# A two-layer graph-attention kernel on one core: the order of work on each engine is read from a sorted table of places instead of from a planner that uses such a table as priorities

## The chip, the cores and the metric

One core of one Trainium2 chip runs the program. The metric is the time of one execution in microseconds (us), on the device. The engines of a core work side by side, each through its own list of instructions in order: TensorE (PE, with PEld for its weight loads), VectorE (DVE), ScalarE (ACT), GpSimd (POOL) and SyncE (SP). SP and POOL here do little but issue transfers (DMA).

## The reference

The input `x` holds 32 graphs of 512 nodes with 512 features, and `adj` their 512 x 512 adjacency. Two attention layers follow each other, all in float32:

```python
def gat_layer(x, mask, W, a_src, a_dst, bias, concat):
    xl = (x @ W).reshape(B, N, H, F)
    asrc = jnp.einsum('bnhf,hf->bnh', xl, a_src)
    adst = jnp.einsum('bnhf,hf->bnh', xl, a_dst)
    e = jax.nn.leaky_relu(asrc[:, :, None, :] + adst[:, None, :, :], 0.2)
    e = jnp.where(mask[..., None], e, -1e9)
    attn = jax.nn.softmax(e, axis=1)
    out = jnp.einsum('bsdh,bshf->bdhf', attn, xl)
    out = out.reshape(B, N, H * F) if concat else out.mean(axis=2)
    return out + bias

h = jnp.maximum(_layernorm(x, axis=-1), 0.0)
mask = (adj > 0) | jnp.eye(N, dtype=bool)[None]
h = jax.nn.elu(gat_layer(h, mask, W1, att_src1, att_dst1, b1, concat=True))    # 4 heads of 256
return x + gat_layer(h, mask, W2, att_src2, att_dst2, b2, concat=False)        # 1 head of 512
```

## The kernel before

The kernel works on one graph after the other and overlaps them: while one graph goes through its second layer, the next goes through the first and the one after that is loaded and normalised. A loop over the graphs (`for i in range(B - 1)`, L1611) records jobs for such a **turn**; 28 of the turns consist of the same 470 jobs each. What stands before them is the start, what stands behind is the end. Nothing is issued while jobs are recorded: `Program.add` only notes for each job its engine, a cost in us and the earlier jobs it depends on, which it derives from the buffers read and written. At the end `Program.emit` issues them in the sequence that `Program.order` returns, and that sequence sets each engine's list.

Most of the matrix products are cut into two by two blocks and done with seven products instead of eight; one of the seven products of the first projection is cut once more. That is why there are many sums and differences on VectorE (`hs`, `hs4`, `t`, `hx`, `wx`, and others in place), and why results pass between PSUM banks by ScalarE copies (`mm<-mm`).

The names that the steps use:

- `mm`: the eight PSUM banks. `ht`: the normalised graph, transposed; `w1_sb`, `w2_sb`: the weights. `xl`, `xl2`: the projected features of layer one and two.
- `as`: the source scores of all nodes on every partition. VectorE transposes them out of `z` (`as<-z`), SP writes them to DRAM (`das<-as`) and reads them back on all partitions (`as<-das`). ScalarE then makes the scores `l<-as,z`, VectorE masks them (`l<-l,mt`) and ScalarE takes their exponentials with sums (`l<-l,low`).
- `rr`: what normalises them goes the same way (`drr<-rr`, `rr<-drr`). VectorE makes `p<-rr,z` from it, GpSimd adds the mask from DRAM by a transfer that accumulates (`p<-dm`), and ScalarE takes `p<-p,z`, the attention weights that TensorE reads.
- `h`: the output of layer one. ScalarE copies it out of a bank with the bias (`h<-mm,b_sb`), VectorE adds the other bank, `xr<-h` and `h<-xr,h` make the ELU.
- `x`: four tiles of the next graph, with `stats<-x` on VectorE; they also serve as scratch for three of the sums of layer two. `t`: four scratch tiles, the residual input and the output of layer two.

The list of an engine is fixed when the program is built. `Program.order` before the change plays the jobs through: it holds each engine's free time, the two transfer queues with their speeds, alone and side by side (`KIND`, `MASK`), the delays between engines (`PAIRS`, `CROSS`, `SAME`), and whenever an engine is free in this play it takes, of the jobs that are ready by then, the one with the smallest rank. The ranks are the numbers of `PLACES` in hundredths of a us, one for each of 2374 jobs: those of the start, of one turn and of the end. A job of turn i has the rank of its place plus i times TensorE's work of a turn. `LATE`, extra lateness of single transfers, is an empty table.

Of the kernel before, what the change touches and what calls it, by code (L numbers as in the profile page):

```python
# [44 lines left out]
class Banks(Slots):  # L45
# [17 lines left out]
PLACES = (  # L63
# [153 lines left out]
)  # L217
LATE = {
   
}  # L220


class Program:
# [7 lines left out]
    CROSS, SAME = 0.15, 0.07  # L231
# [43 lines left out]
    def kind(self, j):  # L275

        if self.jobs[j][0] == "POOL":
            return self.MASK
# [1431 lines left out]
```

## Time and profile before

| | |
|---|---|
| Time, median of 3 runs | 2771.11 us (2768.26 to 2773.03) |
| Profiled execution, its own time | 2769.33 us |
| Its span, first to last instruction | 2767.6 us |
| Instructions | 42320 |
| Transfers | 502.14 MB, 181 GB/s over the span |
| Granted TensorE clock | 0.999 of full |

The span runs from the first to the last instruction, and the execution's own time is 1.7 us longer. Of TensorE's matmuls a weight load (PEld) and a matmul (PE) stand in the profile each; a product in float32 is two of them. Their ends are modelled and overlap the next one's start, so the busy share of PE is nearly 1 also where short pauses are hidden; how far apart the starts are, and how many stand in a stretch, tells more.

The page's largest groups are matmuls, with a mean of 367 to 388 ns each; VectorE's and ScalarE's operations on 128x512 take 681 to 742 and 716 to 721 ns. The chain that ended last is TensorE's for 13% of the span and does not reach back to the start, so I read waits and single places rather than the chain.

### The profile page before, as it was taken

The numbers are of one execution on the slowest core, as the hardware profiler recorded it, in microseconds if no ns is written. First come the engines' busy times: TensorE is split into PE (matmuls) and PEld (weight loads), VectorE is DVE, ScalarE is ACT, GpSimd is POOL, SyncE is SP. The second block draws the span as 40 slices with busy tenths as digits, with TensorE's granted clock in tenths as the row PEclk, the third lists the DMA queues.
The fourth block names the chain that finished last, engine by engine and source line by source line (L and its number), as shares of the span: only waits on it lengthen the run. The fifth ranks groups of instructions, "written<-read, shape, count | busy, mean of one in ns | idle before, by whom it ended". The sixth has DMA issues, their size and how long they took to land. (4 is left out here: it accounts for less than half of the span.)

```text
span 2767.6 us, 42320 instructions
## 1 busy us (share of the span) xinstructions
PE 2742.4 (99%) x12924; PEld 2371.8 (86%) x12924; DVE 2558.2 (92%) x6732; ACT 2229.1 (81%) x4907; POOL 313.1 (11%) x356
## 2 busy tenths in 40 slices
PE   7999999999999999999999999999999999999999
PEld 6788888888888888888888888888888888888887
DVE  8999999999999999999999999999999999999996
ACT  5978888778887788877888877888778788788883
POOL 0110111101111111111011111111111111101110
PEclk9999999999999999999999999999999999999999
DMA  8657766667666667667676766766676767767563
GB/s 232 176 157 182 203 167 184 187 176 194 182 183 179 182 176 196 178 175 195 173 201 172 182 187 178 192 186 180 180 188 175 201 167 180 195 165 208 162 171 112
DMA packets 375864, 502.14 MB, mean 181 GB/s; under 512 B 222804, under 2 KB 227668, under 8 KB 375636
## 3 DMA queue, kind: packets, MB, share of 16 engines
q1 hardware_dynamic: 329844, 332.68, 42.4%
q0 software_dynamic: 45792, 166.74, 25.1%
q8 instruction: 103, 1.69, 0.3%
q14 instruction: 125, 1.02, 0.1%
HBM read 316.41 MB, written 51.31 MB: 133 GB/s over the span
## 5 line engine op out<-in xcount | busy, mean ns | idle before, releaser
L531 PE MATMUL mm<-w_sb,hs 128*128 128x257 f32 (+3 forms) x2908 | 667.0, 367 | 5.1 <-ACT mm L514 3.3
L531 PEld LDWEIGHTS mm<-w_sb,hs 128*128 128x128 f32 x2908 | 539.7, 190 | 87.7 <-ACT mm L514 6.7
L525 POOL DMA_DIRECT2D p<-dm x314 | 273.2, 875 | 2295.0 <-DVE p L517 764.3
L531 PE MATMUL mm<-w_sb,ht 128*128 128x258 f32 x2112 | 528.6, 382 | 2.7 <-ACT mm L514 2.5
L531 PE MATMUL mm<-p,xl 128*128 128x258 f32 (+1 forms) x1984 | 495.8, 383 | 0.1
L531 PE MATMUL mm<-w_sb,h 128*128 128x257 f32 x2056 | 477.8, 379 | 0.0
L517 DVE SCALAR_TENSOR_TENSOR p<-rr,z 128x512 f32<-128x512 f32 (+1 forms) x636 | 456.0, 742 | 2.4 <-DMA rr<-drr 2.4
L531 PEld LDWEIGHTS mm<-w_sb,ht 128*128 128x128 f32 x2112 | 393.7, 190 | 63.6 <-ACT mm L514 6.4
L514 ACT ACTIVATE p<-p,z 128x512 f32<-128x512 f32 (+1 forms) x636 | 433.4, 720 | 17.7 <-DVE p L517 12.4
L531 PEld LDWEIGHTS mm<-w_sb,h 128*128 128x128 f32 x2056 | 389.0, 189 | 58.4 <-ACT xl L514 0.5
L531 PEld LDWEIGHTS mm<-p,xl 128*128 128x128 f32 x1984 | 367.2, 190 | 52.7 <-issue 6.0
L514 ACT ACTIVATE mm<-mm 128x257 f32<-128x257 f32 (+2 forms) x498 | 169.8, 347 | 269.2 <-PE mm L531 236.2
L514 ACT ACTIVATE l<-as,z 128x512 f32<-128x512 f32 x516 | 354.4, 716 | 30.8 <-DMA as<-das 30.7
L514 ACT ACTIVATE l<-l,low 128x512 f32<-128x512 f32 x516 | 370.3, 721 | 7.6 <-DVE low L517 6.7
L517 DVE CUSTOM_DVE_ANT_1 l<-l,mt 128x512 f32<-128x512 f32 x516 | 346.2, 681 | 28.4 <-ACT l L514 27.4
L514 ACT ACTIVATE xl<-mm 128x258 f32<-128x258 f32 (+2 forms) x748 | 269.3, 382 | 91.4 <-PE mm L531 89.8
L514 ACT ACTIVATE h<-mm,b_sb 128x256 f32<-128x256 f32 (+1 forms) x504 | 231.0, 480 | 77.3 <-PE mm L531 76.6
L531 PE MATMUL mm<-t,hs 128*128 128x258 f32 (+1 forms) x992 | 246.1, 380 | 0.0
L517 DVE TENSOR_TENSOR xl<-xl,mm 128x258 f32<-128x258 f32 x372 | 155.3, 419 | 57.9 <-PE mm L531 48.3
L531 PEld LDWEIGHTS mm<-t,hs 128*128 128x128 f32 x992 | 185.8, 190 | 25.5 <-DVE t L517 0.2
L531 PE MATMUL mm<-xl,p 128*128 128x258 f32 (+2 forms) x752 | 189.7, 388 | 1.0 <-ACT h L514 0.6
L517 DVE SCALAR_TENSOR_TENSOR h<-xr,h 128x512 f32<-128x512 f32 x256 | 172.2, 683 | 6.1 <-ACT xr L514 6.1
(137 smaller groups left out, 3706.2 us busy)
## 6 DMA issues: line engine op xcount, KB each, us to landing
p<-dm POOLq DMA_DIRECT2D x314, 512.0 KB, 5.0
rr<-drr SPq DMA_DIRECT2D x159, 512.0 KB
x<-in_x_dram SPq DMA_DIRECT2D x129, 256.0 KB
adj<-in_adj_dram SPq DMA_DIRECT2D x128, 256.0 KB
as<-das SPq DMA_DIRECT2D x64, 512.0 KB
t<-in_x_dram SPq DMA_DIRECT2D x124, 256.0 KB
out_dram<-t SPq DMA_DIRECT2D x124, 256.0 KB
dm<-m SPq DMA_DIRECT2D x64, 256.0 KB
```

The source lines that it names most:

```text
L514: prog.add("ACT", cost, reads, writes, lambda: nc.scalar.activation(*a, **k))
L517: prog.add("DVE", cost, reads, writes, lambda: f(*a, **k))
L525: lambda: nc.gpsimd.dma_start(to, at, accum_op=OP.add), size,
L531: f(*a, **k)
```

## The change

The jobs, their number, what they compute, their buffers and dependencies are the same. `PLACES` has 2374 new numbers, in ten-thousandths of a us. `Program.order` no longer plays anything through: each engine's list is its jobs sorted by rank, whether they are ready or not, and the lists are merged into one sequence for issuing in which no job stands before one that it depends on. The constants of the play and `LATE` are gone. The title of the change calls the numbers "searched anew under deep random delays of the transfers".

```diff
 PLACES = (
-    -21124, -21123, -21187, -21124, -19956, -19941, -19942, -21301, -19903, -19904, -18841, -19897, -6146, 6511,
...
+    -2780662, -2779541, -2728086, -2727982, -2726907, -2665895, -2666659, -2727775, -2192040, -2195819,
...
-LATE = {
...
-}
...
     def ranks(self):
...
-            rank.append(PLACES[v] / 100 + turn * i)
...
+                yield PLACES[j] / 10000
+            elif j < last:
+                yield PLACES[first + (j - first) % each] / 10000 + turn * ((j - first) // each + 1)
+            else:
+                yield PLACES[first + each + j - last] / 10000 + turn * ((last - first) // each + 1)
 
     def order(self):
-        jobs, rank = self.jobs, self.ranks()
...
+        jobs, rank, done = self.jobs, list(self.ranks()), []
+        after, left = [[] for _ in jobs], [len(job[2]) for job in jobs]
         for j, job in enumerate(jobs):
             for d in job[2]:
                 after[d].append(j)
...
-            while soon[e] and soon[e][0][0] <= t:
-                k = heappop(soon[e])[1]
-                heappush(ready[e], (rank[k], k))
-            j = heappop(ready[e])[1]
-            self.start[j] = t
-            free[e] = t + jobs[j][1]
+        lines = {e: [] for e in self.ENGINES}
+        for j in sorted(range(len(jobs)), key=lambda j: (rank[j], j)):
+            lines[jobs[j][0]].append(j)
+        lines = [deque(q) for q in lines.values()]
+        while any(lines):
+            q = min((q for q in lines if q and not left[q[0]]), key=lambda q: rank[q[0]])
+            j = q.popleft()
             done.append(j)
...
+            for k in after[j]:
+                left[k] -= 1
         return done
```

Half of TensorE's jobs stand at most one job from where they stood in its list, half of ScalarE's at most two and half of VectorE's at most three; the farthest have moved by 25, 41 and 65. Line numbers in the new file are 45 lower. Three places follow, all of them turns in the middle of the run. A row is line, operation, output<-inputs with buffer numbers, and shape; `x2` behind a row means twice.

**Place A**, the turn around 850 us: ScalarE's list where the scores `l<-as,z` of a new pair of heads begin. Before:

```order
L514 ACTIVATE h1_82<-mm0_132,b1_sb_75 128x256
L514 ACTIVATE h1_82<-mm6_138,b1_sb_75 128x256
L514 ACTIVATE l1_100<-as1_113,z1_126 128x512
L514 ACTIVATE l2_101<-as1_113,z1_126 128x512
L514 ACTIVATE l0_99<-as1_113,z1_126 128x512
L514 ACTIVATE mm5_137<-mm3_135 128x129
L514 ACTIVATE mm2_134<-mm1_133 128x258
L514 ACTIVATE xr0_96<-h1_82 128x512
```

In the change:

```order
L469 ACTIVATE xr1_97<-h1_82 128x512
L469 ACTIVATE xr2_98<-h1_82 128x512
L469 ACTIVATE mm5_137<-mm3_135 128x129
L469 ACTIVATE h1_82<-mm0_132,b1_sb_75 128x256
L469 ACTIVATE l0_99<-as1_113,z1_126 128x512
L469 ACTIVATE l1_100<-as1_113,z1_126 128x512
L469 ACTIVATE l2_101<-as1_113,z1_126 128x512
L469 ACTIVATE mm2_134<-mm1_133 128x258
L469 ACTIVATE mm0_132<-mm3_135 128x258
```

TensorE's list at the same place, where `mm3` and `mm1` are the banks that those copies read. Before:

```order
L531 MATMUL mm3_135<-w1_sb_73,hs_83 128x129
L531 MATMUL mm7_139<-w1_sb_73,hx5_86 128x129
L531 MATMUL mm1_133<-w1_sb_73,ht_81 128x258 x2
L531 MATMUL mm6_138<-p0_102,xl_79 128x256 x2
L531 MATMUL mm2_134<-p0_102,hs_83 128x256 x2
L531 MATMUL mm3_135<-wx5_85,hs_83 128x129
L531 MATMUL mm6_138<-p0_102,xl_79 128x256 x2
L531 MATMUL mm3_135<-w1_sb_73,ht_81 128x258 x2
L531 MATMUL mm2_134<-w1_sb_73,ht_81 128x258 x2
```

In the change:

```order
L486 MATMUL mm0_132<-p0_102,xl_79 128x256 x2
L486 MATMUL mm6_138<-p0_102,xl_79 128x256 x2
L486 MATMUL mm3_135<-wx5_85,hs_83 128x129
L486 MATMUL mm2_134<-p0_102,hs_83 128x256 x2
L486 MATMUL mm1_133<-w1_sb_73,ht_81 128x258 x2
L486 MATMUL mm3_135<-w1_sb_73,ht_81 128x258 x2
L486 MATMUL mm6_138<-p0_102,xl_79 128x256 x2
L486 MATMUL mm1_133<-w1_sb_73,hs_83 128x258 x2
L486 MATMUL mm2_134<-w1_sb_73,ht_81 128x258 x2
```

The copy `mm5<-mm3` stood behind three `l<-as,z` and stands ahead of them; the short product that fills `mm3` and one with `p` and `hs` moved ahead of the product into `mm1`.

**Place B**, the turn around 1000 us: ScalarE's list where layer two takes its exponentials, four rows `p<-p,z` of which the masks came in two transfers. Before:

```order
L514 ACTIVATE mm7_139<-mm0_132 128x258
L514 ACTIVATE p0_102<-p0_102,z1_126 128x512 x2
L514 ACTIVATE h1_82<-mm6_138,b1_sb_75 128x256
L514 ACTIVATE xr2_98<-h1_82 128x512
L514 ACTIVATE p0_102<-p0_102,z1_126 128x512 x2
L514 ACTIVATE mm2_134<-mm5_137 128x129
L514 ACTIVATE f0_92<-mm5_137 128x129
L514 ACTIVATE xl_79<-mm0_132 128x258
```

In the change:

```order
L469 ACTIVATE xr0_96<-h1_82 128x512
L469 ACTIVATE p0_102<-p0_102,z1_126 128x512
L469 ACTIVATE mm7_139<-mm0_132 128x258
L469 ACTIVATE h1_82<-mm5_137,b1_sb_75 128x256
L469 ACTIVATE p0_102<-p0_102,z1_126 128x512 x3
L469 ACTIVATE xr2_98<-h1_82 128x512
L469 ACTIVATE f0_92<-mm5_137 128x129
L469 ACTIVATE mm2_134<-mm5_137 128x129
L469 ACTIVATE xl_79<-mm0_132 128x258
```

The four stood as two pairs and stand as one and three; `xr` moved behind them, and the copy into `f` ahead of that into `mm2`.

**Place C**, the turn around 880 us: the load of a new `x2` may start when TensorE has read the old one, and VectorE's `BN_STATS` waits for it. TensorE's list before:

```order
L531 MATMUL mm0_132<-xl2_80,p1_103 128x256 x2
L531 MATMUL mm1_133<-w2_sb_74,h1_82 128x257 x4
L531 MATMUL mm0_132<-x2_90,p1_103 128x256 x2
L531 MATMUL mm4_136<-x2_90,p1_103 128x256 x2
L531 MATMUL mm5_137<-xl2_80,hs_83 128x256 x2
L531 MATMUL mm7_139<-xl2_80,hs_83 128x256 x2
L531 MATMUL mm2_134<-w2_sb_74,h1_82 128x257 x4
```

In the change:

```order
L486 MATMUL mm0_132<-xl2_80,p1_103 128x256 x2
L486 MATMUL mm7_139<-xl2_80,hs_83 128x256 x2
L486 MATMUL mm1_133<-w2_sb_74,h1_82 128x257 x4
L486 MATMUL mm5_137<-xl2_80,hs_83 128x256 x2
L486 MATMUL mm4_136<-x2_90,p1_103 128x256 x2
L486 MATMUL mm0_132<-x2_90,p1_103 128x256 x2
L486 MATMUL mm2_134<-w2_sb_74,h1_82 128x257 x4
```

The two products that read `x2` stand behind the two `mm5` and `mm7` with `hs`, which stood behind them. VectorE's list there, before:

```order
L517 SCALAR_TENSOR_TENSOR t3_109<-mm7_139,rs_87,t3_109 128x256
L517 SCALAR_TENSOR_TENSOR p0_102<-rr0_114,z1_126 128x512
L517 TENSOR_TENSOR hs_83<-hs_83,h1_82 128x1024
L517 ISA l1_100,low1_130<-l1_100,mt0_110 128x512
L517 ISA low1_130 128x1
L517 SCALAR_TENSOR_TENSOR p0_102<-rr0_114,z1_126 128x512 x2
L517 BN_STATS stats1_124<-x2_90 128x6
L517 ISA l0_99,low0_129<-l0_99,mt0_110 128x512
L517 ISA low0_129 128x1
L517 BN_AGGR stats1_124<-stats1_124 128x2
L517 SCALAR_TENSOR_TENSOR t1_107<-mm4_136,rs_87,t1_107 128x256
```

In the change:

```order
L472 ISA l0_99,low0_129<-l0_99,mt0_110 128x512
L472 ISA low0_129 128x1
L472 SCALAR_TENSOR_TENSOR t1_107<-mm4_136,rs_87,t1_107 128x256
L472 SCALAR_TENSOR_TENSOR p0_102<-rr0_114,z1_126 128x512
L472 BN_STATS stats1_124<-x2_90 128x6
L472 BN_AGGR stats1_124<-stats1_124 128x2
L472 TENSOR_SCALAR stats1_124<-stats1_124 128x4
L472 SCALAR_TENSOR_TENSOR t2_108<-mm0_132,rs_87,t2_108 128x256
L472 SCALAR_TENSOR_TENSOR p0_102<-rr0_114,z1_126 128x512
L472 TENSOR_TENSOR hs_83<-h1_82,hs_83 128x1024
```

One of the rows `p<-rr,z` stands ahead of `BN_STATS`, where there were more; the long `hs` sum ahead of it (another one of that kind follows in both) and a masking of scores (`l`, ISA) have moved.

More of the change, by code (lines that the diff above doesn't have):

```diff
@@ L2 @@
 from contextlib import ExitStack
-from heapq import heappop, heappush
 import concourse.bass as bass
@@ L305, in order @@
                 after[d].append(j)
-        left = [len(job[2]) for job in jobs]
-        ready_at, self.start, done = [0.0] * n, [0.0] * n, []
-        free, soon, ready = dict.fromkeys(self.ENGINES, 0.0), defaultdict(list), defaultdict(list)
-        wires, now, behind = {"SP": deque(), "POOL": deque()}, 0.0, {"SP": 0.0, "POOL": 0.0}
-        for j in range(n):
-            if not left[j]:
-                heappush(soon[jobs[j][0]], (0.0, j))
-        def release(j, at):
-            for s in after[j]:
-                ready_at[s] = max(ready_at[s], at(s))
-                left[s] -= 1
-                if not left[s]:
-                    heappush(soon[jobs[s][0]], (ready_at[s], s))
@@ L321, in step @@
-        def step(until):
-            nonlocal now
-            busy = [q for q in wires if wires[q] and wires[q][0][1] <= now]
-            speed = dict.fromkeys(wires, 1.0)
-            if len(busy) == 2:
-                speed["SP"], speed["POOL"] = self.kind(wires["SP"][0][0])[2:]
-            event, which = until, None
-            for q in wires:
-                if wires[q]:
-                    j, since, todo = wires[q][0]
-                    t = now + todo / speed[q] if q in busy else since
-                    if t < event:
-                        event, which = t, q
-            for q in busy:
-                wires[q][0][2] -= (event - now) * speed[q]
-                behind[q] -= (event - now) * speed[q]
-            now = event
-            if which in busy:
-                j = wires[which].popleft()[0]
-                release(j, lambda s: event + self.kind(j)[1] + LATE.get(self.place[j], 0) / 100)
-            return which is not None
```

50 lines of the change are left out of this document (removed), and 347 rows, old and new, of the table PLACES.

## The prediction

> **What bounds the kernel now.** I read the totals first, then a table of long stretches, then the waits in the middle of the run, then single places in the timeline.
>
> The page's busy times and the table by stretches (start:end, length, then for each engine busy us and instructions, then granted clock, DMA share, GB/s):
>
> ```profile
> PE 2742.4 (99%) x12924; PEld 2371.8 (86%) x12924; DVE 2558.2 (92%) x6732; ACT 2229.1 (81%) x4907; POOL 313.1 (11%) x356
> ...
> 0.00:86.00 86.00, 71.45 (x318) 58.39 (x319) 73.70 (x293) 53.79 (x122) 8.26 (x14) 0.98 0.80 224
> ...
> 172.00:430.00 258.00, 256.54 (x1219) 223.43 (x1218) 238.56 (x622) 211.18 (x464) 29.76 (x34) 1.00 0.68 183
> 430.00:1204.00 774.00, 771.07 (x3669) 672.62 (x3668) 721.80 (x1878) 636.29 (x1403) 87.88 (x99) 1.00 0.68 182
> 1204.00:1892.00 688.00, 688.00 (x3280) 601.37 (x3279) 645.73 (x1682) 569.39 (x1258) 78.13 (x88) 1.00 0.68 183
> 1892.00:2494.00 602.00, 600.64 (x2855) 523.21 (x2854) 562.78 (x1466) 489.67 (x1080) 69.17 (x78) 1.00 0.69 183
> 2494.00:2666.00 172.00, 171.93 (x817) 149.48 (x817) 159.89 (x411) 144.80 (x321) 19.59 (x23) 1.00 0.66 175
> 2666.00:2768.00 102.00, 96.74 (x411) 76.53 (x409) 75.20 (x186) 49.84 (x111) 7.80 (x9) 0.99 0.48 139
> ```
>
> TensorE is the bound. From 1204 to 1892 us it has no idle time at all, at full clock, and issues 3280 matmuls in 688.00 us, 0.2098 us each. That is its pace when nothing disturbs it, and the order cannot make it shorter, since every matmul stays. A busy share hides short slips, because matmuls overlap in the records; the count does not. At that pace 3669 matmuls need 769.6 us where 774 were used (4.4 lost), 2855 need 598.9 of 602 (3.1 lost), 1219 need 255.7 of 258 (2.3 lost) and 817 need 171.4 of 172 (0.6 lost). **So 10.4 us is all that the middle of the run can give back**; the rest is the start and the end.
>
> Who takes those 10.4 us? The waits between 430 and 2494 us (engine, line, what it waited for: us in total, times, longest):
>
> ```profile
> ACT l L514 <- DMA as<-das: 25.6, 28, 2.3
> ...
> PEld mm L531 <- ACT mm L514: 9.1, 14, 1.6
> ...
> ACT p L514 <- DMA p<-dm: 4.6, 7, 1.4
> PE mm L531 <- ACT mm L514: 4.0, 7, 1.2
> ```
>
> TensorE waits almost only for ScalarE's copies between PSUM banks (`mm<-mm`), and ScalarE in turn waits for two kinds of transfer. Here are all the large ones (ScalarE's timeline: start, length, instruction, in brackets the wait before it):
>
> ```profile
> 256.65 1.95 ACT L514 ACTIVATE l<-as,z 128x512 f32<-128x512 f32 x3 [1.89 <-DMA as<-das]
> 743.58 1.34 ACT L514 ACTIVATE p<-p,z 128x512 f32<-128x512 f32 x2 [0.59 <-DMA p<-dm]
> 852.53 1.95 ACT L514 ACTIVATE l<-as,z 128x512 f32<-128x512 f32 x3 [2.27 <-DMA as<-das]
> 854.38 0.52 ACT L514 ACTIVATE mm<-mm 128x129 f32<-128x129 f32 x2
> 1000.46 1.33 ACT L514 ACTIVATE p<-p,z 128x512 f32<-128x512 f32 x2 [1.37 <-DMA p<-dm]
> 1193.99 1.33 ACT L514 ACTIVATE l<-as,z 128x512 f32<-128x512 f32 x2 [1.86 <-DMA as<-das]
> 1958.08 1.33 ACT L514 ACTIVATE l<-as,z 128x512 f32<-128x512 f32 x2 [1.82 <-DMA as<-das]
> 2274.66 1.33 ACT L514 ACTIVATE p<-p,z 128x512 f32<-128x512 f32 x2 [0.54 <-DMA p<-dm]
> 2360.10 1.33 ACT L514 ACTIVATE p<-p,z 128x512 f32<-128x512 f32 x2 [0.64 <-DMA p<-dm]
> ```
>
> And what the worst `as` wait does to TensorE, with the transfer's issue (SyncE's and TensorE's timeline):
>
> ```profile
> 846.49 0.33 SPq L520 DMA_DIRECT2D as<-das  x1
> ...
> 850.90 1.03 PE L531 MATMUL mm<-p,xl 128*128 128x256 f32 x4
> 851.76 1.03 PE L531 MATMUL mm<-p,hs 128*128 128x256 f32 x4
> 852.63 0.39 PE L531 MATMUL mm<-wx,hs 128*128 128x129 f32 x2
> 852.85 1.03 PE L531 MATMUL mm<-p,xl 128*128 128x256 f32 x4
> 854.69 2.01 PE L531 MATMUL mm<-w_sb,ht 128*128 128x258 f32 x8 [0.81 <-ACT mm L514]
> ```
>
> A group of four matmuls lasts 0.87 us from start to start (850.90, 851.76, 852.63), so the one at 852.85 was issued by 853.72, and the next began at 854.69: 0.97 us lost. ScalarE had to finish three `l<-as,z` before the copy at 854.38 that TensorE needed. The wait was 2.27 us and 0.97 got through, so this place (**place A**) swallows 1.3 us; its four large waits (1.89, 2.27, 1.86, 1.82) cost 7.84 - 4 x 1.3 = 2.6 us. At **place B**, the `p<-p,z` pair of the second layer, the pair and its copy run without a gap into TensorE's need, so nothing is swallowed: 0.59 + 1.37 + 0.54 + 0.64 = 3.1 us. The other 10.4 - 2.6 - 3.1 = 4.7 us are slips too small for a row, spread over 28 turns.
>
> **The change part by part.** No instruction is added or removed. `LATE` is empty before, so dropping it does nothing. What changes is which work of a turn stands ahead of which, on all engines.
>
> *Place A.* The bank copy `mm5<-mm3`, behind the three `l<-as,z` before, now stands two rows ahead of them, so the wait no longer reaches the matmul at 854.69. The next copy behind them, `mm2<-mm1`, has its matmuls 1.95 us later (two groups of 0.87 and one of two short ones pass ahead), and its reader starts two groups, 1.74 us, after those. Counted from 850.90 that reader starts at 854.6; less 0.2 us for the step from ScalarE to TensorE and 0.3 for the copy, the copy may start at 854.1, so the three must begin by 854.1 - 1.95 = 852.2. Before, by the same steps from 853.72, it was 853.3 - 1.95 = 851.3. That is 0.9 us more. On VectorE the transpose `as<-z` that starts the transfer has 0.94 us less work ahead of it (recorded durations of what passed it), so the transfer can start up to as much sooner. Together up to 1.8 us, where the worst wait got through by 0.97. I take **-2.6 us**, all four; bounds 0 and -2.6.
>
> *Place B.* Before, two `p<-p,z` stand directly ahead of the copy TensorE needs; now three stand together, with an `xr` and one `f` copy between. The earliest that needs the second half of `p` must start 2 x 0.61 + 0.52 + 0.16 = 1.9 us ahead of the copy, where it was 1.2: 0.7 us sooner. VectorE's last write of `p` comes 0.2 us sooner. The place thus has about 0.5 us **less** for its transfer. The four waits stay and grow by 0.5 each, +2.0 at worst; but the matmuls that read those copies have gained a third of a microsecond of room (next part), which takes 1.3 of it back. I take **+0.7 us**; bounds -1 and +4.
>
> *The small slips.* For every matmul group of a turn in the middle I took its recorded start minus the recorded end of the last VectorE or ScalarE instruction that feeds it, added the TensorE work that the new order puts ahead of the group and took off the work that it puts ahead of the feeder, all at recorded durations. Of 166 such rooms in a turn, 15 to 21 are under 0.3 us before, the tightest under 0.2. In 21 of the 28 turns none is under 0.3 in the new order, the tightest being 0.34; in six one or two are 0.12 to 0.24, where the record itself was disturbed, and in the first turn two fall below zero, by 0.6 and 0.1. So a late feeder of 0.1 to 0.3 us, which now moves TensorE, should no longer do so. I take **-4.5 us** of the 4.7; bounds 0 and -4.7, and +0.7 for the first turn on the worse side.
>
> *Start and end.* The start depends on these rows:
>
> ```profile
> 12.06 2.82 PE L531 MATMUL mm<-identf,x 128*128 128x128 f32 x12 [12.06 <-ACT x L514]
> ...
> 13.21 0.43 DVE L517 SCALAR_TENSOR_TENSOR xr<-w_sb,p 128x256 f32<-128x256 f32 x1 [1.30 <-DMA p<-in_L_gnn_att_dst_dram]
> ...
> 14.67 5.92 PE L531 MATMUL mm<-w_sb,ht 128*128 128x258 f32 x24
> ```
>
> The first product with weights (14.67) follows VectorE's sums, which waited for the attention vector until 13.21. That transfer is the tenth on SyncE's queue in both orders, behind the same nine, so moving the x loads to the front does not move 14.67. All four `x` now pass ScalarE before the first copy of `ht`, which may add 0.3. The end (2666 on) is a new permutation of the same chain: 0, bounds -3 and +3 for both ends together.
>
> The sum is -2.6 + 0.7 - 4.5 = **-6.4 us** against the profiled execution's own 2769.33 us (span 2767.6): 2762.9. That execution lies 1.8 us under the median of the three timed runs, 2771.11; the same sum on the median gives 2764.7. The timed runs with more disturbance have more to give back, so I stay with the first: I forecast **2763**.
>
> **Where the order gives less room.** Not all transfers gain. The load of the next `x` rows on SyncE:
>
> ```profile
> 784.57 0.34 SPq L520 DMA_DIRECT2D x<-in_x_dram  x1
> 789.20 0.69 DVE L517 BATCH_NORM_STATS2 stats<-x 128x6 f32<-128x512 f32 x1 [0.85 <-DMA x<-in_x_dram]
> ...
> 880.26 0.39 SPq L520 DMA_DIRECT2D x<-in_x_dram  x1
> ...
> 886.11 0.69 DVE L517 BATCH_NORM_STATS2 stats<-x 128x6 f32<-128x512 f32 x1
> ...
> 895.88 0.42 DVE L517 TENSOR_TENSOR xl<-xl,mm 128x257 f32<-128x257 f32 x1 [0.87 <-PE mm L531]
> ```
>
> One such load took 789.20 - 784.57 = 4.6 us; another was given 5.85 us and was not waited for. In the new order the last matmuls that read the old `x2` stand two groups, 1.7 us, later, and VectorE has 1.5 us less work ahead of the statistics: the load at 880.26 is left with 2.7 us. VectorE will wait there, 1 to 1.9 us in every turn. Queued behind it are the bank sums for the next product (`hs`, a reader six microseconds away) and the `xl2` sums, which already wait for TensorE (the 0.87 at 895.88) and stand 1.6 us sooner now, so 2.5 us of wait hides there. I cost it at nothing; without that cover it is 1 us a turn.
>
> The Trainium skill (DMA: Bandwidth & Descriptors, Anatomy of one DMA) fits a transfer as 2.0 us plus its bytes at 436 GB/s, for GpSimd's path. By an estimate from that, 256 KB take 2.6 us, the load just fits and no wait appears. The 4.6 us measured here disagree, and the measurement decides.
>
> **The rivals.**
>
> *Slower: VectorE's new wait reaches TensorE.* It decides once the wait for `x` exceeds the 2.5 us of cover, or if the cover is gone because the `xl2` sums no longer wait. Then VectorE, 92% busy, passes 1 us a turn on: 28 turns make +28, less the 6.4, on 2769: 2791. Against it: the cover, and VectorE's 645.73 of 688.00, 5.3 us idle in 86. Chance 0.10.
>
> *Nothing: the losses only move.* Place B's 0.5 us less decides, with more of its 28 transfers late; A's 2.6 saved go into B's bound of +4, and the small slips come back at other rows because the tightest new steps (0.39 us from matmul through ScalarE to matmul, beside the copy itself) are as short as the shortest in this trace. 2769 to 2772, say 2770. Chance 0.25.
>
> *More: nearly all 10.4 us come back,* and the start and end give 3 to 5: 2756. For it speaks the tightest room of 0.34. Against it, place B. Chance 0.15.
>
> **How the numbers follow.** The forecast has 0.50, itself within 2759 to 2767. A measurement here tells 0.2% from no change, 5.5 us: faster means under 2765.6. Of the forecast case four fifths lie below that (0.41), all of the third rival (0.15) and a sixth of the second (0.04): faster 0.60. Slower is the first rival and a hint of the second: 0.11. Same 0.29. The range reaches from 2755, just under the third rival, past the second's 2772 to 2774; the slow rival and a little of each edge lie outside.
>
> **What would show it.** Right: no `l<-as,z` wait of ScalarE that ends at a TensorE wait; place B still there; a count of matmuls per us of 0.2098 in more of the stretches; VectorE waiting for `x` in every turn. Wrong: TensorE waiting for VectorE's `hs` or `h` each turn, ScalarE's `p<-dm` waits grown well over 4.6 us, or the first weight product after 15.5 us.

## The result, and the profile after

| | before | changed |
|---|---|---|
| Time, median of 4 runs | 2769.69 us (2764.25 to 2773.03) | 2798.07 us (2795.65 to 2799.97) |
| Ratio to before, 95% interval | | 1.0104 (1.0084 to 1.0124) |
| Profiled execution: its time, its span | 2769.33 us, 2767.6 us | 2796.34 us, 2794.6 us |

The change makes the kernel 1.04% slower, by 28 us. Forecast was 2763, 6 us faster, with a range that ended at 2774. Direction and size are both wrong.

The page of the changed kernel, busy time per engine and the group that changed most, then the same group before (line, engine, operation, shapes, count | busy, mean ns | idle time just before and who ended it):

```profile
PE 2748.7 (98%) x12924; PEld 2374.3 (85%) x12924; DVE 2567.6 (92%) x6732; ACT 2229.6 (80%) x4907; POOL 312.2 (11%) x356
...
L486 PE MATMUL mm<-w_sb,hs 128*128 128x257 f32 (+3 forms) x2908 | 673.7, 368 | 21.7 <-ACT f L469 21.5
```

```profile
L531 PE MATMUL mm<-w_sb,hs 128*128 128x257 f32 (+3 forms) x2908 | 667.0, 367 | 5.1 <-ACT mm L514 3.3
```

The shares are within a point of those of before; what is new is one releaser, ScalarE's copy `f`, which ends 21.5 us of TensorE's idle time. The stretches of the prediction again (stretch, length, busy PE, PEld, DVE, ACT, POOL with counts, clock, DMA share, GB/s):

```profile
430.00:1204.00 774.00, 763.97 (x3619) 665.82 (x3618) 714.80 (x1856) 626.22 (x1379) 86.89 (x98) 1.00 0.68 180
1204.00:1892.00 688.00, 683.75 (x3252) 596.38 (x3251) 642.52 (x1665) 563.67 (x1241) 78.85 (x89) 1.00 0.69 182
1892.00:2494.00 602.00, 596.18 (x2826) 519.82 (x2826) 558.41 (x1448) 489.61 (x1078) 68.22 (x77) 1.00 0.68 181
```

From 1204 to 1892 us TensorE issued 3280 matmuls before and issues 3252 now, with 4.25 us of idle time where it had none. A loss that is the same in an undisturbed stretch is no late transfer; something waits once per turn. The waits of the whole span (engine, line, what it waited for: us in total, times, longest):

```profile
PEld mm L486 <- ACT f L469: 27.1, 29, 4.0
PE mm L486 <- ACT f L469: 21.5, 28, 3.8
...
ACT p L469 <- DMA p<-dm: 15.5, 20, 3.1
...
DVE stats L472 <- DMA x<-in_x_dram: 5.1, 4, 2.4
...
ACT l L469 <- DMA as<-das: 2.1, 4, 0.6
```

28 waits for 28 turns. One of them, in an undisturbed turn (timeline of the changed kernel: start, length, instruction, in brackets the idle time before it and its releaser):

```profile
1096.95 0.39 PE L486 MATMUL mm<-wx,hx 128*128 128x129 f32 x2
...
1097.02 0.62 ACT L469 ACTIVATE xr<-h 128x512 f32<-128x512 f32 x1
1097.54 0.27 ACT L469 ACTIVATE f<-mm 128x129 f32<-128x129 f32 x1
...
1097.87 0.49 PE L486 MATMUL mm<-w_sb,hs 128*128 128x129 f32 x2 [0.53 <-ACT f L469]
```

`mm<-wx,hx` is the fifth product of the small inner cut and fills 129 columns of a PSUM bank; `mm<-w_sb,hs` is the first, and goes into the 129 columns beside them in the same bank (called the two halves here). They start 0.22 us apart when nothing stands between them (1088.88 and 1089.10 in a run below). Here they are 0.92 us apart, because ScalarE, after its `xr`, first copies the one half into `f`. So 0.70 us are lost here, as in 25 of the 28 turns; in the other three it is more. In a list of the built program with each instruction's waits, the row shows why: the wait is in the program. Before and in the change, a middle turn:

```
L531 MATMUL mm_137<-wx_85,hx_86 128x129
L531 MATMUL mm_137<-w_sb,hs 128x129

L486 MATMUL mm_137<-wx_85,hx_86 128x129 [waits Activation_49]
L486 MATMUL mm_137<-w_sb,hs 128x129 [waits Activation_49]
```

The wait of the second row is the one for `f`. The order of TensorE's two products is the same in both kernels. What the change turned round is ScalarE's `f<-mm` and the half copy `mm<-mm` behind it. The half copy needs the product, so while it stood first the product was issued ahead of both. With `f` first, `f` is also issued ahead of the product, and the program then makes the product wait for it, since both use one bank.

### The profile page after: what moved, and what is told of

It is laid out like the page before. It is cut to its first block, busy times and chain, and to the rows that moved or that the text cites. A ratio compares the mean times of both kernels' runs of the same rounds, so it can differ in the third digit from the quotient of the medians.

```text
span 2794.6 us, 42519 instructions
## 1 busy us (share of the span) xinstructions
PE 2748.7 (98%) x12924; PEld 2374.3 (85%) x12924; DVE 2567.6 (92%) x6732; ACT 2229.6 (80%) x4907; POOL 312.2 (11%) x356
## 5 line engine op out<-in xcount | busy, mean ns | idle before, releaser
L486 PE MATMUL mm<-w_sb,hs 128*128 128x257 f32 (+3 forms) x2908 | 673.7, 368 | 21.7 <-ACT f L469 21.5
L486 PE MATMUL mm<-p,xl 128*128 128x258 f32 (+1 forms) x1984 | 506.6, 384 | 0.0
L469 ACT ACTIVATE p<-p,z 128x512 f32<-128x512 f32 (+1 forms) x636 | 435.5, 715 | 30.7 <-DMA p<-dm 15.5
L472 DVE CUSTOM_DVE_ANT_1 l<-l,mt 128x512 f32<-128x512 f32 x516 | 338.5, 682 | 57.7 <-ACT l L469 57.6
L472 DVE TENSOR_TENSOR xl<-xl,mm 128x258 f32<-128x258 f32 x372 | 146.6, 415 | 50.4 <-PE mm L486 46.4
```

The costliest lines, as they stand in the source:

```text
L469: prog.add("ACT", cost, reads, writes, lambda: nc.scalar.activation(*a, **k))
L472: prog.add("DVE", cost, reads, writes, lambda: f(*a, **k))
L486: f(*a, **k)
```

## The experiments

Times are medians. Each run was compared with runs of the kernel before on the same chip, whose medians were 2767.7 to 2768.9.

| run | us | ratio to before, 95% interval |
|---|---|---|
| product issued first | 2771.54 (2769.59 to 2778.73) | 1.0016 (1.0007 to 1.0024) |
| half copy first | 2772.35 (2769.02 to 2776.14) | 1.0016 (1.0007 to 1.0024) |
| before, with `f` first | 2797.99 (2792.44 to 2801.75) | 1.0106 (1.0093 to 1.0119) |
| `p<-rr,z` early | 2770.92 (2762.68 to 2781.39) | 1.0008 (0.9996 to 1.0019) |
| start and end | 2771.38 (2769.14 to 2774.55) | 1.0011 (1.0003 to 1.0020) |
| `xr` first | 2768.97 (2764.57 to 2776.82) | 1.0005 (0.9996 to 1.0013) |
| both | 2769.57 (2766.97 to 2774.07) | 1.0001 (0.9992 to 1.0010) |
| both, ScalarE's start | 2768.24 (2766.48 to 2773.77) | 1.0003 (0.9994 to 1.0012) |
| stall ladder | 2959.81 (one run) | |
| two seams | 2770.09 (2768.53 to 2771.73) | 1.0009 (1.0000 to 1.0018) |
| start of before | 2768.09 (2765.30 to 2771.02) | 0.9999 (0.9990 to 1.0008) |
| second seam later | 2770.22 (2767.65 to 2775.92) | 1.0008 (0.9999 to 1.0017) |

**The product issued first.** One number of the 2374 is changed, the place of the product `mm<-w_sb,hs`. It was behind that of `f` (1440854) and is now just behind that of `mm<-wx,hx` (1438585). TensorE's list has these two neighbours in either case, and every engine's list is that of the changed kernel; on TensorE the built programs differ in 28 waits for ScalarE.

```diff
-    1525529, 1622205, 1623505, 1628094, 1627944, 1413217, 1419309, 1421872, 1427609, 1438585, 1440854, 1455100,
+    1525529, 1622205, 1623505, 1628094, 1627944, 1413217, 1419309, 1421872, 1427609, 1438585, 1440854, 1438590,
```

> The changed kernel with one number of the table: in each turn the first weight product of the small inner cut (mm<-w_sb,hs, 128x129) is issued ahead of ScalarE's copy f<-mm, not behind it. Each engine's own order stays word for word that of the changed kernel; only 28 waits of TensorE for ScalarE fall away. Theory W (TensorE waits in each of the 28 turns for a copy that it does not need, because the copy stands ahead of it in the issued sequence): the 28 stalls of 0.69 us go, and with them the 1.27, 3.25 and 2.10 us by which late masks lengthened three of them, of which a part comes back at the next product: 2798 - 19 - 0 to 9 = 2770 to 2779, and no wait of a w_sb,hs product for f is left. Rival P (the loss is in the places of the operations on ScalarE and VectorE, and TensorE would wait as long for the half copy that follows): the stall moves two products on, and the time stays at 2793 to 2800.

Measured 2771.54: 26.5 of the 28 us are gone. Against the kernel before, run beside it, it is still 0.16% slower (0.07 to 0.24). The group of this run shows no wait for `f` any more:

```profile
L486 PE MATMUL mm<-w_sb,hs 128*128 128x257 f32 (+3 forms) x2908 | 670.2, 367 | 0.1
```

And the same place in its timeline:

```profile
1088.88 0.39 PE L486 MATMUL mm<-wx,hx 128*128 128x129 f32 x2
...
1088.95 0.62 ACT L469 ACTIVATE xr<-h 128x512 f32<-128x512 f32 x1
...
1089.10 0.39 PE L486 MATMUL mm<-w_sb,hs 128*128 128x129 f32 x2
...
1089.52 0.28 ACT L469 ACTIVATE f<-mm 128x129 f32<-128x129 f32 x1
```

The product starts 0.22 us after its neighbour. Now `f` is the one that comes after: 0.03 us behind the product's end. In no turn of this run, of the changed kernel or of the kernel before did the two overlap (`f` at least 0.04 us after the product, or the product 0.05 us after `f`, from the recorded times of all 28 turns). So the expectation was wrong in one word: it is not a wait that TensorE "does not need". One of the two must wait for the other, and the sequence of issue decides which. ScalarE has time to spare there, TensorE has not. The Trainium skill (PSUM — Partial Sum Buffer, PSUM bank collisions raise a hardware error) states a rule that fits: two engines must not use one bank in the same partitions at once, disjoint columns included, and the compiler's scheduler adds a dependency between any two instructions on different engines that do. No run here let the two overlap, so what would happen then is not shown; the waits in the built programs are as that section says.

**The half copy first.**

```diff
-    1525529, 1622205, 1623505, 1628094, 1627944, 1413217, 1419309, 1421872, 1427609, 1438585, 1440854, 1455100,
-    1441202, 1457306, 1457303, 1473100, 1470406, 1484061, 1470403, 1484600, 1492200, 1503101, 1503114, 1503200,
+    1525529, 1622205, 1623505, 1628094, 1627944, 1413217, 1419309, 1421872, 1427609, 1438585, 1441202, 1455100,
+    1440854, 1457306, 1457303, 1473100, 1470406, 1484061, 1470403, 1484600, 1492200, 1503101, 1503114, 1503200,
```

> The changed kernel with two numbers of the table exchanged: on ScalarE the half copy mm<-mm goes ahead of the copy f<-mm in each turn, as it stood before the change; the other engines' orders stay. Theory W: the half copy needs the product, so the product is issued ahead of both copies, the wait is not made, and the time is that of the run that only issues the product earlier, within 3 us: 2770 to 2779. Rival P: 2793 to 2800. If ScalarE's order between the two copies mattered by itself, this run and the other would differ by over 5 us.

Measured 2772.35, 0.8 us from the run above. ScalarE's order between the two copies costs nothing by itself; what it does to the sequence of issue cost 26 us.

**Before, with `f` first.** The same thing done to the kernel before, at this one place, after its planner has made the lists:

```diff
+        lines = [deque(j for j in done if jobs[j][0] == e) for e in self.ENGINES]
+        held = {}
+        first, last = self.marks[1], self.marks[-2]
+        for j in range(first, last, self.marks[2] - first):
+            f, w, c = j + 123, j + 124, j + 125
+            q = lines[self.ENGINES.index("ACT")]
+            if q.index(c) < q.index(f):
+                q.remove(f)
+                q.insert(q.index(c), f)
+            held[w] = f
...
+            ok = [q for q in lines if q and not left[q[0]] and held.get(q[0], -1) in out]
```

> The kernel before with this one thing done to it in each of the 28 turns: f<-mm goes ahead of the half copy on ScalarE, and the w_sb,hs product is issued behind f. The other engines' orders stay. Theory W: f comes after two exponentials there and ends about 0.95 us after the place where the product starts now (86.9 against 85.95 in one turn), so a stall of 0.7 to 1.0 us in each turn: 2770 + 20 to 28 = 2790 to 2798. Rival P: the kernel before loses nothing by it beyond 3 us: 2768 to 2773.

Measured 2797.99, as slow as the changed kernel. Its group:

```profile
L552 PE MATMUL mm<-w_sb,hs 128*128 128x257 f32 (+3 forms) x2908 | 668.4, 368 | 26.4 <-ACT f L535 23.7 <-DVE hs L538 1.3 <-ACT mm L535 0.9
```

The wait for `f`, put in, takes 28 stalls of 0.59 to 1.6 us, some 28 in all, from the starts of the two products; the ratio moved by 0.0106. The usual stall is longer here, 0.94 us instead of 0.70. One cause, taken out of one kernel and put into the other, moves the time by nearly the whole of what was to be explained.

**`p<-rr,z` early.** What follows is about the rest, the 8 us between 2771.5 and the forecast. VectorE's list in one turn, with the wait for `f` removed as in the first run:

```diff
 L472 SCALAR_TENSOR_TENSOR p_103<-rr_115,z_125 128x512
 L472 TENSOR_TENSOR p_102<-p_102 128x2x256
-L472 TENSOR_TENSOR hs<-xl 128x256
+L472 SCALAR_TENSOR_TENSOR p_103<-rr_115,z_125 128x512 x3
+L472 TENSOR_TENSOR hs<-xl 128x256
+L472 TENSOR_TENSOR hs<-xl,hs 128x256
 L472 TENSOR_TENSOR t_108<-p_102,t_107 128x512
 L472 TENSOR_TENSOR xl<-xl 128x2x128
-L472 SCALAR_TENSOR_TENSOR p_103<-rr_115,z_125 128x512
-L472 TENSOR_TENSOR hs<-xl,hs 128x256
-L472 SCALAR_TENSOR_TENSOR p_103<-rr_115,z_125 128x512 x2
```

> The first run of this set, with seven operations of VectorE exchanged in each turn: the four products p<-rr,z that the masks are added to move ahead of two sums, a difference and an addition (hs, xl, t), so that the second mask transfer p<-dm is issued about 2 us sooner and has that much more room before ScalarE's exponentials. Theory L (what is then left over of the late p<-dm, waits of 15.5 us in 20 places, still reaches TensorE): these waits fall below 5 us and the time by 2 to 6 us against the first run of the set. Rival: the late transfers are late by their own cause and cost TensorE nothing once the wait is gone, or the operations moved back are late for TensorE themselves: within 2 us of the first run, or slower.

A miss. The waits for `p<-dm` fell to 11.5 us in 16 places, not below 5, and the runs spread from 2762.7 to 2781.4, the lowest and the highest of all runs without the wait for `f`. In the profiled execution, the slowest of the twelve, two turns went wrong where none had (timelines of this run, SyncE, then ScalarE, then TensorE):

```profile
1587.72 2.85 SPq L766 DMA_TRANSPOSE x<-adj  x1
```

```profile
1600.90 1.34 ACT L469 ACTIVATE ht<-x 128x1024 uint16<-128x1024 uint16 x1 [7.12 <-DMA x<-adj]
```

```profile
1603.35 1.65 PE L486 MATMUL mm<-p,xl 128*128 128x256 f32 x3 [7.13 <-DVE h L472]
```

The masks, issued about 2 us earlier, now travel beside the transposes `x<-adj`, which have 4.67 us from issue to use in an undisturbed turn of the changed kernel and are waited for there only when late. One was 7 us late, and TensorE stood for 7.1 us. That the two transfers collide is my reading, and it is not shown: in the run **both** below, where the masks stand where the change has them, the same transfer was late in the same turn (ScalarE's timeline of that run):

```profile
1596.00 1.34 ACT L469 ACTIVATE ht<-x 128x1024 uint16<-128x1024 uint16 x1 [3.88 <-DMA x<-adj]
```

TensorE stood for 3.5 us there. So a late `x<-adj` costs several microseconds where it comes, and moving the masks towards it gained nothing; whether the move made it late is open.

**Start and end.** Four places on VectorE, each outside the repeated turns (shown is the first: the addition that empties the bank of the product at 214 us).

```diff
+L472 TENSOR_TENSOR xl_80<-xl_80,mm_132 128x257
 L472 TENSOR_TENSOR xl_80<-xl_80,mm_138 128x257
 L472 TENSOR_TENSOR xl_80<-xl_80,mm_135 128x257
...
 L472 TENSOR_TENSOR hs<-hs,xl 128x256 x2
-L472 TENSOR_TENSOR xl_80<-xl_80,mm_132 128x257
```

> The changed kernel without the wait for f (as in the first run: the product is issued first), and with four places of VectorE exchanged outside the repeated turns: the addition that empties the bank of the stalled product at 214 us (xl2) moves ahead of two other additions, the addition x2 at 2696 us ahead of the operations for rr, and at 2782 us the masks of the first chunk ahead of those of the second. Theory S (what the new order loses against the prediction, once the wait is gone, lies at the start and the end, where the prediction costed nothing): the stalls of 2.82, 0.88 and 0.67 us go, nothing else moves: 4.4 us under the first run's 2771.5, so 2765 to 2769, below the kernel before. Rival: they are covers for what is late behind them, the next feeder stalls TensorE as long, and the time stays within 1.5 us of 2771.5.

Measured 2771.38: the rival. The stall at 214 us went, and at the next group but two another stood in its place, of nearly the same length, for another engine (timeline of this run):

```profile
217.94 1.14 PE L486 MATMUL mm<-t,hs 128*128 128x258 f32 x4
221.49 1.50 PE L486 MATMUL mm<-t,hs 128*128 128x256 f32 x4 [2.41 <-ACT mm L469]
```

**`xr` first**, and **both**. On ScalarE, in every turn, without the wait for `f`:

```diff
-L469 ACTIVATE p_102<-p_102,z_127 128x512 x3
-L469 ACTIVATE xr_98<-h_82 128x512
+L469 ACTIVATE p_102<-p_102,z_127 128x512
+L469 ACTIVATE xr_98<-h_82 128x512
+L469 ACTIVATE p_102<-p_102,z_127 128x512 x2
 L469 ACTIVATE f_92<-mm_137 128x129
```

> The changed kernel without the wait for f, and in each turn ScalarE's exponential xr<-h goes ahead of the two exponentials p<-p,z that wait for the second mask transfer; no transfer and no other engine's order moves. Theory B (what is left in the middle, 1.06, 2.96, 0.63 and 0.58 us at four turns and the slow products behind the longest, is the late p<-dm, and ScalarE's 0.62 us of other work ahead of it hides that much of each): 1.5 to 3 us under the first run, 2768 to 2770, with fewer waits of p for p<-dm than 15.8 us in 18 places. Rival: VectorE's sum over p, now 0.6 us later in every turn, is late for TensorE: 0 to 8 us above the first run.

> Both edits together: the changed kernel without the wait for f, the four places at the start and the end, and xr<-h ahead of the two exponentials. If both theories hold they add: 2771.5 - 4.4 - 1.5 to 3 = 2763.5 to 2766, faster than the kernel before (2768.9) by about 0.15%, and near the 2763 that was predicted for the change. If one falls, the time is that of the other alone.

2768.97 and 2769.57. The first is 2.6 us under the run without it, as the theory had it, though the two intervals overlap; the waits for `p<-dm` hardly changed (15.2 us in 17 places). The two edits did not add.

**ScalarE's start.** Ahead of the first turn, `ht<-x` and two exponentials go behind the half copy (not shown: in the last turn one `h<-mm` goes ahead of an exponential):

```diff
-L469 ACTIVATE ht<-x_90 128x2x4x128
+L469 ACTIVATE mm_137<-mm_136 128x256
 L469 ACTIVATE p_104<-p_104,z_126 128x512 x2
-L469 ACTIVATE mm_137<-mm_136 128x256
...
 L469 ACTIVATE ht<-x_91 128x2x4x128
+L469 ACTIVATE ht<-x_90 128x2x4x128
```

> The run with both edits, and three operations of ScalarE moved: ahead of the first turn the copy ht<-x (1.33 us, first read 11.9 us later) and two exponentials go behind the half copy that TensorE then waited for (the stall of 2.57 us at 219 us to which the one at 214 us had moved), and in the last turn h<-mm goes ahead of an exponential (0.70 us). Theory S2 (the stall at the start has two feeders in a row, VectorE's addition and ScalarE's half copy, and goes once both are early): 2.57 falls to about 0.5 us, the last to under 0.2, 2 to 3 us under the 2769.6 of both edits: 2766 to 2768. Rival (a third feeder stands behind the second): within 1 us of 2769.6.

2768.24, and in the timeline the loss has moved once more, to a third and a fourth feeder:

```profile
222.18 1.13 PE L486 MATMUL mm<-p,xl 128*128 128x258 f32 x4 [1.37 <-DVE p L472]
224.50 1.86 PE L486 MATMUL mm<-p,hs 128*128 128x256 f32 x4 [1.18 <-ACT ht L469]
```

2.82 us at one place became 2.57 at the next and 1.53 + 1.34 at two more. There the start is short of work done in time on VectorE and ScalarE alike, and none of the exchanges tried mends it. One middle stretch of this execution, though, is what the prediction had promised:

```profile
1204.00:1892.00 688.00, 688.00 (x3281) 601.35 (x3281) 649.25 (x1686) 570.26 (x1259) 77.81 (x88) 1.00 0.69 183
```

**The stall ladder.** It measures what a stall of TensorE costs beyond its own length, by repeating the copy `f` of the changed kernel.

```diff
-                act(HALF, [tk + (1,)], [ek], e, tt[:, hi], AF.Copy)
+                halves.append(q)
+                more = 4 * (max(len(halves) // 2 - 1, 0) // 4) if len(halves) % 2 else 0
+                prog.add(
+                    "ACT", HALF, [tk + (1,)], [ek],
+                    lambda: [nc.scalar.activation(e, tt[:, hi], AF.Copy) for _ in range(1 + more)],
+                )
```

> The changed kernel with its wait for f, in which ScalarE repeats the copy f<-mm of the waited-for place: 4 more copies from turn 4 on, 8 from turn 8, and so on up to 24 from turn 24, about 0.17 us each. It measures the cost of a stall of TensorE by its length: 0.7, 1.4, 2.1, 2.7, 3.4, 4.1 and 4.8 us, four turns each. Theory H (a stall above some 2.9 us is followed by several us of products at half the clock, as behind the stalls of 2.91 and 4.05 us of the changed kernel): none behind 0.7 to 2.1, all or most behind 3.4 and more, with 1.4 to 2.7 us of loss each, so the time is 2798 + 57 + 20 to 35 = 2875 to 2890. Rival (the slow products had another cause that happened to fall there): the stalls alone, 2850 to 2860, and no halved clock behind them.

Four more copies lengthened the stall by 1.25 us (I had guessed 0.7), so the steps were 0.70, 1.94, 3.2, 4.4, 5.7, 6.9 and 8.2 us and the time 2959.81, above the 2875 to 2890 expected. What was expected of the slow products holds. Behind stalls up to 1.94 us only the first product is slow, by 0.10 us. Of three stalls of 3.19 to 3.34 us one cost nothing more and two cost 1.78 and 2.90. All 18 of 4.4 us and more cost 1.5 to 3.0, mean 2.3. The clock stands behind it (stretches after a stall of 1.94, two of 3.19 and one of 4.44 us; the number behind POOL's count is the granted clock):

```profile
754.50:757.50 3.00, 1.85 (x11) 1.73 (x12) 0.89 (x2) 2.02 (x8) 0.00 (x0) 1.00 0.13 51
934.70:938.40 3.70, 3.60 (x12) 3.15 (x13) 0.40 (x2) 1.44 (x5) 0.00 (x0) 0.56 0.00 0
1117.00:1120.70 3.70, 3.56 (x21) 3.29 (x22) 1.65 (x5) 1.89 (x7) 0.00 (x0) 1.00 0.01 3
1482.20:1488.00 5.80, 5.78 (x19) 5.06 (x20) 1.79 (x6) 1.39 (x4) 0.00 (x0) 0.50 0.07 17
```

**Seams.** Three runs join lists: the kernel before's start (its lists up to the second turn), the mended turns of the run with ScalarE's start, and one of the two ends. The table then holds start times from the traces of these two kernels, with a row per job of start, a turn and end, and the issue goes by them:

```diff
-            if j < first:
-                yield PLACES[j] / 10000
-            elif j < last:
-                yield PLACES[first + (j - first) % each] / 10000 + turn * ((j - first) // each + 1)
+            if j < first + each:
+                yield PLACES[j] / 1000
+            elif j < last - each:
+                yield PLACES[first + each + (j - first) % each] / 1000 + 84.7 * ((j - first) // each - 1)
```

> Each engine's order is that of the kernel before up to the second repeated turn and from the 28th on, word for word, and in between that of the run with the start of ScalarE mended (the changed kernel's turns, without the wait for f and with xr<-h first). The sequence of issue is by start times. Theory S3 (the change's turns are as good as predicted once the wait is gone, 84.70 us almost throughout against a median of 84.94, and what cancels that is its start, 3.4 us later at the first turn's small inner cut, 235.8 against 232.4, and its end, 232.7 against 230.3): the time is the kernel before's less the 12.2 us that its turns lose against 84.7 and plus 3 to 6 that the new turns lose to late masks and the two seams: 2768.5 - 12.2 + 3 to 6 = 2759 to 2763. Rival (the late masks and what they bring decide, wherever the start and the end come from): 2766 to 2770.

> Each engine's order is that of the kernel before up to the second repeated turn, and from there on, the end included, that of the run with ScalarE's start mended; so one seam, at the start, and none at the end. Theory S4 (what the run with two seams lost, 88.0 us in the turn of the second seam against 84.7, was the seam): 3.3 us come back, 1.8 go to the changed kernel's longer end (232.7 against 230.9): 2770.1 - 1.5 = 2768 to 2769, within the kernel before's spread. Rival (the turn of 88.0 us was a late transfer of that one execution): 2770 to 2772.

> As the run with two seams, with the second seam one turn later: all 27 middle turns are the mended ones, and only what lies behind the last turn has the kernel before's order. Theory S4 (a seam costs what the orders of both sides don't fit, and it fits better where the turn's own work has been finished): the 3.3 us of the second seam shrink to 0 to 2 us, 2767 to 2769. Rival: the seam moves on with its loss, 2770 to 2772.

2770.09, 2768.09 and 2770.22. The start and most of the end came back as expected, but with two seams the last middle turn took 88.00 us instead of 84.70. Without the second seam that turn took 85.80 and the time is 2 us lower, though the two intervals overlap; with the seam one turn on, the last middle turn took 84.70 and the end was no shorter. None of the twelve is faster than the kernel before by anything that can be measured; the best, at 2768.09, equals it.

## Why the prediction was wrong

A product that stands at the same place in every turn, `mm<-wx,hx` from above, divides each profiled execution into three. Its first and its last occurrence in the kernel before:

```profile
232.39 0.39 PE L531 MATMUL mm<-wx,hx 128*128 128x129 f32 x2
...
2530.99 0.39 PE L531 MATMUL mm<-wx,hx 128*128 128x129 f32 x2
```

And in the changed kernel:

```profile
233.59 0.39 PE L486 MATMUL mm<-wx,hx 128*128 128x129 f32 x2
...
2554.76 0.39 PE L486 MATMUL mm<-wx,hx 128*128 128x129 f32 x2
```

| profiled execution, us | start | 27 turns | an undisturbed turn | turns, above 27 of these | end | span |
|---|---|---|---|---|---|---|
| before | 232.4 | 2298.6 | 84.68 | 12.2 | 236.6 | 2767.6 |
| changed | 233.6 | 2321.2 | 85.50 | 12.7 | 239.8 | 2794.6 |
| product issued first | 234.8 | 2297.0 | 84.70 | 10.1 | 238.4 | 2770.2 |
| both, ScalarE's start | 235.8 | 2292.6 | 84.70 | 5.7 | 238.1 | 2766.5 |

Of the 27.0 us between the first two spans, 22.6 lie in the turns, and 27 x 0.82 = 22.1 of those are the same in every turn: the 0.70 of the stall, 0.10 for a slow product behind it, and 0.02 that the new turn takes longer anyway. Start and end make 1.2 + 3.2. The 5.7 of the last row is the best of the nine runs with mended turns; in the others the same column has 8.4 to 12.7.

**What bounds the kernel** was right. TensorE's pace of 0.2098 us held, and in the mended run it issued 3281 matmuls in 688.00 us where the prediction counted 3280.

**The step that failed is "the small slips".** There the prediction took "its recorded start minus the recorded end of the last VectorE or ScalarE instruction that feeds it" for 166 places of a turn, found the tightest room at 0.34 us and concluded that no late feeder would move TensorE. All 166 are feeders by data. `f` does not feed the product; it reads the other half of its bank, and the recorded dependencies keep the halves apart by separate keys. So the room that decided, 0.70 us short in every turn, was not in the list. The prediction even quoted the rows ("three stand together, with an `xr` and one `f` copy between") and counted `f` as 0.16 us of ScalarE's time. The Trainium skill's rule on banks, named above, speaks of just this, and the prediction did not draw on it. For the feeders the step did look at, the direction was right, but its 4.5 us are not shown: 15 of 27 turns are within 0.02 us of the shortest once the wait is gone, 10 of 27 before. Leaving out the tenth turn, where the masks are late (below), the turns lose 3.0 to 8.3 us in the nine runs with mended turns, against 10.5 before. Most of those runs have more changed than the wait, so this gain can't be put down to one term.

**Place A** was right: the waits for `as<-das` are 2.1 us in 4 places (25.6 in 28 places between 430 and 2494 us before), and none is among TensorE's stalls over 0.3 us.

**Place B** had the right mechanism and was mis-sized, inside its bounds. +0.7 was taken; the waits for `p<-dm` are 15.5 us in 20 places, and standing ahead of `f` they reached TensorE undamped. The worst one (timelines of the changed kernel, ScalarE, then TensorE):

```profile
1007.82 1.33 ACT L469 ACTIVATE p<-p,z 128x512 f32<-128x512 f32 x2 [3.13 <-DMA p<-dm]
1009.06 0.61 ACT L469 ACTIVATE xr<-h 128x512 f32<-128x512 f32 x1
1009.58 0.26 ACT L469 ACTIVATE f<-mm 128x129 f32<-128x129 f32 x1
```

```profile
1005.73 0.39 PE L486 MATMUL mm<-wx,hx 128*128 128x129 f32 x2
1009.89 0.80 PE L486 MATMUL mm<-w_sb,hs 128*128 128x129 f32 x2 [3.77 <-ACT f L469]
```

A transfer that came 3.13 us late made a stall of 3.94 and then halved the clock, so this turn took 91.22 us, 5.7 more than its neighbours; before, the same turn lost 1.7. Without the wait for `f` the four late masks still cost 1.06 + 2.96 + 0.63 + 0.58 = 5.2 us and some 1.6 for slow products, against the 3.1 that the prediction found before: +3.7 in that execution, where it took +0.7 and bounded at +4. With the start and the end this accounts for most of why taking out the wait brings the kernel near to before's time and not below it.

**Start and end** were costed at nothing with bounds of 3. They lost 4.4 in the changed kernel and 3.8 to 6.0 in the six mended runs that keep its start, so this term too fell outside its bounds. The largest piece is the product at 214 us, a stall of 2.83 us; the prediction noted rooms of -0.6 and -0.1 in the first turn, and took 0.7 for them as a bound.

**Place C** was right in its cost and wrong in its step. VectorE waits for `x` in 4 places, not in every turn. The room left to that load came out as 3.53 us in the tightest of 23 middle turns, not 2.7, and it sufficed without a wait as a rule. The 4.6 us that the prediction took as the length of a load was one late load: in the trace before, the same load of the turn had 3.70 us as a rule and was waited for in 2 of 25 middle turns. The Trainium skill's estimate of 2.6 us (DMA: Bandwidth & Descriptors, Anatomy of one DMA), which the prediction set aside for it, gave what happened as a rule: the load fits and no wait appears.

**The rivals.** The slower one had 2791 us, near what came, by another mechanism: VectorE waited for `x` in 4 places, 5.1 us in all, and not in every turn. "Nothing" is what is left once the wait for `f` is out.

**Left open:** why the late masks are late. They recur: the tenth turn, near 1000 us, lost 1.7 us before and 2.6 to 5.7 in the changed kernel and in nine runs of its mended turns, and nothing in the one where the masks went earlier; in the run of the kernel before with `f` first it lost 0.1. I did not try to find the cause.

## What to carry to other kernels

A list of dependencies that is made from data does not hold all waits of the built program: before costing a reordering, compare the waits of the bounding engine's instructions one by one, old program against new, and explain each new one. Where two operations share a bank, the sequence in which they are issued decides which engine waits; put the engine that is the bound first, which here was one number and 26 us. One execution does not give the cause of a late transfer: the one that was late here when another had been moved towards it was late, too, where nothing had been moved.

## What the hardware showed that was not expected

A pause of TensorE of 2.6 us or more can cost more than its length, since the clock is then at one half for some microseconds. Pauses are counted here from one product's start to the next one's. In the changed kernel, after the pause of 4.05 us near 1006 us, and after the one of 3.05 us at 214 us (stretches with the granted clock):

```profile
1010.00:1014.40 4.40, 4.40 (x14) 3.77 (x15) 1.52 (x4) 1.39 (x4) 0.00 (x0) 0.50 0.02 4
```

```profile
217.20:221.00 3.80, 3.73 (x17) 3.27 (x18) 1.40 (x4) 3.79 (x7) 0.00 (x0) 1.00 1.06 273
```

The second kept the full clock. The same pause at the same place in the ladder run did not:

```profile
217.50:221.70 4.20, 4.13 (x11) 3.37 (x12) 1.79 (x4) 3.06 (x5) 0.00 (x0) 0.60 1.06 274
```

In the traces of all runs, between 100 and 2720 us, 12 of the 19 pauses of 2.63 to 3.30 us halved the clock and 7 did not; all 24 of 3.45 us and more did. Single pauses of 1.5 to 2.1 us never did, but two of them close together, 1.75 and 1.56 us in the run with ScalarE's start, did:

```profile
224.60:228.20 3.60, 3.60 (x10) 2.86 (x10) 3.14 (x12) 0.70 (x3) 1.70 (x2) 0.53 0.60 146
```

Behind each of these the half clock lasted 3.41 us, or two or three times as long. The Trainium skill (TensorE: Matmul & The Clock Gate, Part 1: The HAM clock gate) says that the clock falls to half after an idle window of about 3.4 us that runs freely, and comes back after about as long of work. The half clock, its return and the length of its stretches agree. Pauses of 2.63 to 3.30 us, and the two short ones, halved the clock though they are shorter than that window.
